# A six-layer decoder block on one core: the tokens of three groups go to the experts by way of DRAM, and the last pairs' sums use four banks

## The chip, the cores and the metric

The kernel runs on one core of a Trainium2 chip. The metric is device time in microseconds (us) of one execution; the time of a kernel is the median of several runs. The core has a matrix engine (TensorE, in the profile PE, with its weight loads as PEld), three engines for elementwise work (VectorE as DVE, ScalarE as ACT, GpSimd as POOL) and SyncE (SP), whose queue issues most of the DMAs here. Matrix products land in PSUM, which has eight banks of 128 x 512 float32; everything else lives in SBUF (128 partitions) or in DRAM.

## The reference

Two decoder layers on 16 blocks of 128 tokens with 512 features, all in float32. Each layer is self-attention, cross-attention to a context, and a feed-forward part; after each of the six, the result is added to x and a layernorm follows. The change touches the last two of them:

```python
x = _layernorm(x + _L1_xattn_ref(x, ctx_512, Wq, Wkv_expand, Wout))   # 16 heads of 32, causal softmax
x = _layernorm(x + _L1_ffn_ref(x, gate, gate_up, down, shared_gate_up, shared_down))

logits = x @ gate_weight.T                      # 8 experts
topk_w, topk_idx = top_k(softmax(logits), 2)    # two experts for each token
y = sum over the two experts e of w_e * (silu(x @ gate_e) * (x @ up_e)) @ down_e
y = y + (silu(x @ shared_gate) * (x @ shared_up)) @ shared_down
```

## The kernel before

x stays in SBUF as 16 tiles of 128 tokens x 512 features, one for each block b. Four blocks make a group, so there are four groups. A matrix product over features needs x turned, with features on partitions. The kernel has two ways to do that. `transpose_x` (line L124) uses PE: four 128 x 128 transposes into one "mm" bank and one copy by ACT (L129). The class `Turn` (L133 to L154) goes through DRAM: `send` lets ACT write a copy of x with its columns regrouped (L144) and SP write that copy to the DRAM tensor `turned` (L145); `fetch` reads it back in four DMAs (L151), such that each 32-row stripe lands on its partitions; `back` turns the 32 x 32 squares on DVE (L154). Layer 0 and the first attention of layer 1 use `Turn` for some blocks.

**The cross-attention of layer 1** is run by `attend` (L255), a software pipeline over 18 steps n. In step n it makes the scores of block n, applies the value product of block n-2 into a PSUM bank of the tag "pt" and copies it to SBUF as `oT` by ACT (L274). Then for each of four sets of heads it starts the softmax of block n (DVE: mask and maximum, L212 and L214; ACT: four exponentials, L219), finishes an earlier one (DVE reciprocal L225, POOL multiply L226), and turns the weights of block n-1 on PE into a "pt" bank (L231). At the second set, `project_out` (L172) multiplies by the output weights (L176), adds x on DVE (L177) and normalises: statistics on DVE (L111, L113), the inverse root on POOL, and the scaling of x[b] on POOL (L122). In between, `Share.deal` hands out the projections of the next group: on PE `pk`, `pq` and `pv` into two "mm" banks (L165), which are emptied as keys on DVE (L987), as queries `qT` on ACT (L991) and as values `v` on ACT (L996).

**The experts** begin at L1050. Before the router can work, all 16 blocks are turned with `transpose_x` into two tiles that each hold two groups, and SP copies x[b] to the DRAM tensor `sums` (L1054), to which the experts' results are added later. The router's logits of all four groups are accumulated in one bank (L1058); a chain of small DVE operations then gives each token two places in a list sorted by expert (`slot`, and `which`, L1158, the expert of each tile of 128 places). The shared expert's first half, `hidden` (L1102), takes one group at a time: two matrix products (L1116), Silu on ACT (L1123), product on DVE (L1124). After each of these from the second call on, `send` (L1183) copies the rows of one block on ACT (L1189) and scatters them on POOL to their places (L1194). Then 39 tiles of sorted tokens pass through their experts (L1244 to L1277), with the shared expert's second half dealt out between them.

**The end** adds up. Of blocks 8 to 15, the pairs (8,12), (9,13) and (10,14) get their shared product there by `shared_pair` (L1290): ten matmuls over two banks and one short one for each block (L1299, L1307). `add_late` (L1384) adds the experts' sums on DVE, which empties the banks. Blocks 11 and 15 follow one at a time (L165). Statistics, scaling and output follow each.

The order on each engine comes from a scheduler: it places the instructions of the program, unless `keep_in_program_order` fixes them, by its own estimate of when each can run. Once built, each engine takes its queue in that order. A DMA on SP also waits for the one eight places before it in its own ring of eight semaphores.

Of the kernel before, what the change touches and what calls it, by code (L numbers as in the profile page):

```python
# [18 lines left out]
P = 128  # L19
NB = 16  # L20
D = 512
# [25 lines left out]
def decoder_kernel(ctx: ExitStack, tc: tile.TileContext, a: dict, out: bass.AP):  # L47
# [25 lines left out]
    def bank(tag, shape, name):  # L73
        return psum.pool.tile(shape, F32, tag=tag, name=name, bufs=psum.banks[tag])
# [11 lines left out]
    def load_const(name, shape, src, pool=const):  # L86
        t = pool.tile(shape, F32, tag=name, name=name)
        nc.sync.dma_start(t, src)
        return t
# [30 lines left out]
    def layernorm(b, engine=nc.vector):  # L120
        mean, rstd = statistics(b)
        engine.tensor_scalar(x[b], x[b], mean, rstd, ALU.subtract, ALU.mult)  # L122

    def transpose_x(xT, b, at):  # L124

        tr = bank("mm", [P, KC, P], "tr")
        for k in range(KC):
            nc.tensor.transpose(tr[:, k, :], x[b][:, k * P : (k + 1) * P], ident)
        nc.scalar.copy(xT[:, :, at : at + P], tr)  # L129
# [42 lines left out]
    def project_out(oT, wo, b):  # L172

        po = bank("mm", [P, D], "po")
        for c in range(KC):
            nc.tensor.matmul(po, lhsT=oT[:, c, :], rhs=wo[:, c, :], start=(c == 0), stop=(c == KC - 1))  # L176
        nc.vector.tensor_tensor(x[b], x[b], po, ALU.add)  # L177
        layernorm(b, nc.gpsimd)
# [23 lines left out]
    class Softmax:  # L202
# [20 lines left out]
        def finish(self):  # L223
            rs = small.tile([P, 4], F32, tag="rs", name="rs")
            nc.vector.reciprocal(rs, self.sm)  # L225
            nc.gpsimd.tensor_tensor(self.p, self.p, spread(rs, P), ALU.mult)  # L226
# [25 lines left out]
            self.parts = self.part  # L252
            self.deal()

    def attend(pool, mask, wo, prepare, score, value):  # L255


        held = {}
        share = Share(prepare(0), 1)
        share.deal()  # L260
        late = []
        for n in range(NB + 2):
            if n % GB == 0 and n < NB:
                share.rest()
                share = Share(prepare(n // GB + 1), 3 * GB if n + GB < NB else 3 * GB + 6)
            if n < NB:
                sc = [bank("sc", [P, 4, P], "sc") for _ in range(4)]
                score(sc, n)
                held[n] = [Softmax(pool, sc[c], mask) for c in range(4)]
            if n >= 2:  # L270
                av = bank("pt", [P, KC, P], "av")
                value(av, n - 2, [s.pT for s in held.pop(n - 2)])
                oT = pool.tile([P, KC, P], F32, tag="oT", name="oT")
                nc.scalar.copy(oT, av)  # L274
            for c in range(4):
                if n < NB:
                    held[n][c].start()
                    late.append(held[n][c])
                if late and (len(late) > 1 or n >= NB):
                    late.pop(0).finish()  # L280
                if 1 <= n <= NB:
                    held[n - 1][c].turn()
                if c == 1 and n >= 2:
                    project_out(oT, wo, n - 2)
                else:
                    share.deal()


    GB = 4
# [49 lines left out]
    with tc.tile_pool(name="p1", bufs=1) as p1:  # L339
# [5 lines left out]
        wo = p1.tile([P, KC, D], F32, tag="wo", name="wo")  # L345
# [44 lines left out]
        for g in range(2, NG):  # L390
            blocks = slice(g * GB, (g + 1) * GB)
# [90 lines left out]
        def score(sc, n):  # L482
            qkT = groups[n // GB][0]
            toks = slice(n % GB * P, (n % GB + 1) * P)
            for j in range(4):
                for c in range(KV):
                    rows = slice(c * HD, (c + 1) * HD)
                    nc.tensor.matmul(sc[c][:, j, :], lhsT=qkT[rows, j, toks], rhs=qkT[rows, 4, toks], start=True, stop=True)

        def value(av, n, pT):  # L490
            v = groups[n // GB][1]
            for c in range(KV):
                rows = slice(c * HD, (c + 1) * HD)
                nc.tensor.matmul(av[rows], lhsT=v[:, n % GB, rows], rhs=pT[c], start=True, stop=True)

        attend(p1, mask1, wo, prepare, score, value)
        rawp.__exit__(None, None, None)
    pre_pool = tc.tile_pool(name="pre", bufs=2, reuse_waits="tile")
# [198 lines left out]
    with tc.tile_pool(name="p3", bufs=1) as p3:  # L697
# [34 lines left out]
        for g in range(NG):  # L732
            hs = []
            if g + 1 < NG:
                coming, more = inputs(g + 1)
# [31 lines left out]
            for i in range(GB):  # L767
                b = g * GB + i
                po = bank("mm", [P, D], "po")
                for f in range(NF0):  # L770
                    for n in range(2):
                        nc.tensor.matmul(  # L772
                            po, lhsT=hs[f][n][:, i * P : (i + 1) * P], rhs=w3[:, f, :],
# [10 lines left out]
    with tc.tile_pool(name="p4", bufs=1) as p4:  # L784
# [19 lines left out]
        causal = load_const("causal", [P, P], a["causal"], p5w_)  # L804
# [11 lines left out]
        coming = []  # L816
# [120 lines left out]
    with tc.tile_pool(name="p5", bufs=1) as p5:  # L937
# [15 lines left out]
        wq5, wo5 = wqo5[:, 0], wqo5[:, 1]  # L953
# [61 lines left out]
                        start=True, stop=True,  # L1015
                    )

        attend(p5, causal, wo5, prepare, score, value)
    psum.share(mm=2, sc=3, pt=2, av=1)
    p5w.__exit__(None, None, None)  # L1020

# [5 lines left out]
    with tc.tile_pool(name="p6", bufs=1, reuse_waits="tile") as p6:  # L1027
# [6 lines left out]
        def half_rows(g):  # L1034
            return slice(g % 2 * 64, g % 2 * 64 + 64)
# [8 lines left out]
        xTs = []  # L1044
        for g in range(0, NG, 2):
            pair = p6.tile([P, 2, KC, TG], F32, tag="ew", name=f"xT{g}", bufs=3)
            xTs += [pair[:, 0], pair[:, 1]]

        with tc.tile_pool(name="p6a", bufs=1, side="right", reuse_waits="tile") as p6a:


            for b in range(NB):
                transpose_x(xTs[b // GB], b, b % GB * P)
                nc.sync.dma_start(sums[b * P : (b + 1) * P, :], x[b])  # L1054
            plT = bank("av", [P, TG], "plT")
            for k in range(KC):
# [144 lines left out]
        with tc.tile_pool(name="p6r", bufs=1, side="right", reuse_waits="tile") as p6r:  # L1201
# [80 lines left out]
            def shared_down(tasks, b, then):  # L1282
                g, i = divmod(b, GB)
                chain(
                    tasks, "po", [(acts[g][:, m_, i * P : (i + 1) * P], sw_dn[:, m_, :]) for m_ in range(5)]
                    + [(halves[g // 2][half_rows(g), i * P : (i + 1) * P], sw_dn[half_rows(g), 5, :])],
                    lambda po: then(b, po),
                )

            def shared_pair(tasks, pair, then):  # L1290


                got = {}

                def whole(b, m_):
                    g, i = divmod(b, GB)
                    if m_ == 0:
                        got[b] = bank("mm", [P, D], "po")
                    nc.tensor.matmul(  # L1299
                        got[b], lhsT=acts[g][:, m_, i * P : (i + 1) * P], rhs=sw_dn[:, m_, :],  # L1300
                        start=(m_ == 0), stop=False,
                    )

                def last():
                    for b in pair:
                        g, i = divmod(b, GB)
                        nc.tensor.matmul(  # L1307
                            got[b], lhsT=halves[g // 2][half_rows(g), i * P : (i + 1) * P],
                            rhs=sw_dn[half_rows(g), 5, :], start=False, stop=True,
                        )  # L1310
                    for b in pair:
                        then(b, got[b])

                for b in pair:
                    for m_ in range(5):
                        tasks.append((0.86, lambda b=b, m_=m_: whole(b, m_)))
                tasks.append((1.0, last))
# [13 lines left out]
            tasks = []  # L1331
# [55 lines left out]
            for blocks in order:  # L1387
                tasks = []
                if blocks[0] >= EARLY and len(blocks) == 2:
                    shared_pair(tasks, blocks, add_late)  # L1390
                for b in blocks:
                    if b < EARLY:
                        tc.keep_in_program_order(nc.gpsimd.tensor_tensor(x[b], x[b], ys[b], ALU.add))
                    elif len(blocks) == 1:
                        shared_down(tasks, b, add_late)
                for _, run in tasks:
                    run()
                at = slice(0, len(blocks))
                mv = small.tile([P, 2, 2], F32, tag="mv2", name="mv2")
                for i, b in enumerate(blocks):  # L1400
                    st = small.tile([P, 6], F32, tag="st", name="st")
                    tc.keep_in_program_order(nc.vector.bn_stats(st, x[b]))
                    tc.keep_in_program_order(nc.vector.bn_aggr(mv[:, i], st))
                ve = small.tile([P, 2], F32, tag="ve2", name="ve2")
                tc.keep_in_program_order(nc.vector.tensor_scalar(ve[:, at], mv[:, at, 1], EPS, None, ALU.add))
                minus = small.tile([P, 2], F32, tag="minus", name="minus")
                tc.keep_in_program_order(nc.vector.tensor_scalar(minus[:, at], mv[:, at, 0], -1.0, None, ALU.mult))
                if behind:
                    finish(*behind.pop())
                behind.append((blocks, mv, ve, minus))  # L1410
# [126 lines left out]
```

## Time and profile before

| what | value |
|---|---|
| three runs | 2070.22, 2071.18, 2071.78 us; median 2071.18 us |
| the profiled execution | 2073.39 us |
| its span on the core | 2071.6 us |
| granted PE clock, mean | 0.992 of full |
| cross-attention of layer 1 | about 1285 to 1497 us of the span |
| start of the experts, to the first `hidden` at full rate | 1497 to 1520 us |
| tiles of sorted tokens | about 1667 to 2019 us |
| end | 2019 to 2071.6 us |

The profile is one execution. The span is what lies between its first and last instruction on the core; the execution's own time is 1.8 us longer. Rows of a timeline show the start in the span, the duration, engine, line, output and inputs; a bracket gives the idle time of the engine before the row and what ended it. Transposes of one block count as four rows, 128 x 512 matmuls in float32 as two rows each.

### The profile page before, as it was taken

The page shows a single profiled execution, that of the slowest core. Times are in us where ns is not written, and L with a number is a line of the kernel's source. Part 1 is how long each engine was busy: PE and PEld are TensorE (multiplying, and loading weights), DVE is VectorE, ACT ScalarE, POOL GpSimd, SP SyncE. Part 2 cuts the span into 40 slices and gives each one's busy share as a digit, 9 for nine tenths or more (in the row PEclk, how much of TensorE's full clock was granted, in tenths as well). Part 3 has the DMA queues.
Part 4 walks back from the last instruction along what each step waited for, and adds up shares of the span by engine and source line. Part 5 has one row for each costly group of instructions (what it writes and reads, how often), then busy time and mean ns, then how long its engine had stood idle before and what let it go on. Part 6 is the DMA issues. An engine that isn't in the chain of part 4 may idle for free.

```text
span 2071.6 us, 25330 instructions
## 1 busy us (share of the span) xinstructions
PE 2014.1 (97%) x9093; PEld 1115.7 (54%) x9093; DVE 878.6 (42%) x1763; ACT 627.6 (30%) x2107; POOL 646.8 (31%) x674
## 2 busy tenths in 40 slices
PE   8999999999999999999999999999899999999997
PEld 4555554444444458888554445555544455555552
DVE  4777732444554254432134314777731122232234
ACT  3555532333333333222310112766622200000002
POOL 6445530111211113233322113455613222223223
PEclk9999989999999999999999999999999999999999
DMA  9201231344432232001310018500023256786844
GB/s 249 78 25 40 104 124 52 104 127 137 132 117 83 66 118 71 21 11 54 143 51 22 11 34 266 204 22 21 27 66 118 87 141 178 226 237 188 247 108 168
DMA packets 155470, 221.58 MB, mean 107 GB/s; under 512 B 49616, under 2 KB 110416, under 8 KB 150608
## 3 DMA queue, kind: packets, MB, share of 16 engines
q1 hardware_dynamic: 140448, 146.51, 22.6%
q0 software_dynamic: 13792, 72.14, 11.6%
q8 instruction: 72, 1.18, 0.2%
q10 hardware_dynamic: 1104, 1.31, 0.2%
q14 instruction: 54, 0.44, 0.1%
HBM read 182.73 MB, written 72.69 MB: 123 GB/s over the span
## 4 chain that ended last, share of the span: by engine, by line
PE 85%; DMA 5%; DVE 4%; POOL 3%; ACT 2%; issue 1%; SPq 0%; POOLq 0%; DVEq 0%; ACTq 0%
PE po L649 10%; PE po L176 7%; PE pq L590 5%; PE pq L841 5%; PE pq L165 5%; PE pg L1116 4%; PE ry L1265 4%; PE po L772 4%; PE pa L745 4%; PE pb L745 4%; DMA ew<-in_l1f_w_dram,which 4%; PE rg L1244 4%; PE ru L1244 4%; PE pu L1116 3%; PE pv L851 3%; PE av L637 3%
## 5 line engine op out<-in xcount | busy, mean ns | idle before, releaser
L226 POOL TENSOR_TENSOR p<-p,rs 128x512 f32<-128x512 f32 x192 | 200.0, 1043 | 504.0 <-DVE rs L225 494.7
L649 PE MATMUL po<-mT,cc 128*128 128x512 f32 x512 | 231.5, 600 | 0.2 <-ACT cc L642 0.2
L219 ACT ACTIVATE p<-t,nmx 128x128 f32<-128x128 f32 x512 | 198.6, 390 | 34.0 <-POOL p L226 10.2
L649 PEld LDWEIGHTS po<-mT,cc 128*128 128x128 f32 x512 | 95.1, 190 | 114.3 <-issue 106.3
L219 ACT ACTIVATE p<-sc,nmx 128x128 f32<-128x128 f32 x256 | 90.2, 374 | 117.8 <-DVE nmx L214 110.4
L590 PE MATMUL pq<-xT,wqr 128*128 128x512 f32 x256 | 115.7, 593 | 2.9 <-ACT xT L129 2.9
L1214 POOL DMA_INDIRECT ew<-in_l1f_w_dram,which x39 | 40.6, 1042 | 249.1 <-PE ry L1265 182.8
L176 PE MATMUL po<-wo,oT 128*128 128x512 f32 x256 | 116.9, 600 | 0.4 <-ACT qkT L454 0.4
L1249 ACT ACTIVATE rsg<-rg 128x352 f32<-128x352 f32 x39 | 18.1, 464 | 326.4 <-PE rg L1244 310.1
L115 POOL TENSOR_SCALAR ve<-mv 128x1 f32<-128x1 f32 x80 | 18.1, 226 | 303.0 <-DVE mv L113 289.1
L1244 PE MATMUL rg<-ew,xsT 128*128 128x352 f32 x312 | 101.8, 469 | 10.4 <-DMA ew<-in_l1f_w_dram,which 9.6
L841 PE MATMUL pq<-xT,wq 128*128 128x512 f32 x256 | 110.6, 592 | 0.7 <-ACT xT L129 0.7
L1265 PE MATMUL ry<-ew,ractT 128*128 128x512 f32 (+1 forms) x234 | 106.9, 592 | 0.0
L122 POOL TENSOR_SCALAR x<-x,mv,rstd 128x512 f32<-128x512 f32 x48 | 100.5, 2094 | 4.5
L1244 PE MATMUL ru<-ew,xsT 128*128 128x352 f32 x312 | 98.7, 459 | 0.0
L219 ACT ACTIVATION_READ_ACCUMULATOR p<-t,nmx 128x1 f32 x512 | 96.1, 188 | 0.0
L233 DVE COPY pT<-pt 128x512 f32<-128x512 f32 x128 | 86.6, 679 | 19.4 <-PE pt L231 19.4
L756 POOL TENSOR_TENSOR hl<-ht,hh 128x512 fp32r<-128x512 f32 x44 | 57.4, 1306 | 108.2 <-ACT hh L754 108.2
L231 PEld LDWEIGHTS pt<-ident,p 128*128 128x128 f32 x512 | 60.0, 141 | 55.7 <-issue 41.5
L1116 PE MATMUL pg<-xT,sw_gu 128*128 128x512 f32 x192 | 86.5, 593 | 0.0
L1277 POOL DMA_INDIRECT sums<-ry,place x39 | 61.8, 1585 | 74.7 <-DMA sums<-ry,place 37.8
L1251 DVE TENSOR_TENSOR ract<-rsg,ru 128x352 f32<-128x352 f32 x39 | 20.3, 521 | 151.0 <-issue 140.4
(243 smaller groups left out, 3676.4 us busy)
## 6 DMA issues: line engine op xcount, KB each, us to landing
piece<-in_l0f_w_dram SPq DMA_DIRECT2D x48, 352.0 KB
away<-sq SPq DMA_DIRECT2D x32, 512.0 KB
pT<-away SPq DMA_DIRECT2D x128, 128.0 KB
raw<-in_l0x_raw_dram SPq DMA_DIRECT2D x8, 1728.0 KB
slots_x<-zero SPq DMA_DIRECT2D x1, 10023.0 KB
sums<-zero SPq DMA_DIRECT2D x1, 9984.0 KB
xs<-slots_x SPq DMA_DIRECT2D x156, 64.0 KB
x<-turned SPq DMA_DIRECT2D x128, 64.0 KB
```

Of the source, the lines that this page charges most:

```text
L122: engine.tensor_scalar(x[b], x[b], mean, rstd, ALU.subtract, ALU.mult)
L165: nc.tensor.matmul(got["p"], lhsT=lhsT, rhs=rhs, start=(n == 0), stop=(n == len(pairs) - 1))
L176: nc.tensor.matmul(po, lhsT=oT[:, c, :], rhs=wo[:, c, :], start=(c == 0), stop=(c == KC - 1))
L219: nc.scalar.activation(self.p[:, j, :], src[:, j, :], AF.Exp, bias=nmx[:, j : j + 1], accum_out=self.sm[:, j : j + 1])
L226: nc.gpsimd.tensor_tensor(self.p, self.p, spread(rs, P), ALU.mult)
L590: nc.tensor.matmul(pq, lhsT=wqr[:, k, cols], rhs=xT[:, k, :], start=(k == 0), stop=(k == KC - 1))
L649: nc.tensor.matmul(self.po, lhsT=self.cc[:, 4 * par + j, :], rhs=mT[h], start=(par == 0 and j == 0), stop=(par == 1 and j == 3),)
L745: nc.tensor.matmul(dst, lhsT=wt[:, k, f * P : (f + 1) * P], rhs=xs[n][:, k, :], start=(k == 0 and n == 0), stop=(k == KC - 1 and n == 1),)
L841: nc.tensor.matmul(pq, lhsT=wq4[k // 2][:, k % 2, c * P : (c + 1) * P], rhs=xT[:, k, :], start=(k == 0), stop=(k == KC - 1))
L1116: nc.tensor.matmul(dst, lhsT=sw_gu[:, k, at : at + P], rhs=xTs[g][:, k, :], start=(k == 0), stop=(k == KC - 1),)
L1244: nc.tensor.matmul(dst, lhsT=self.xT[:, k, :], rhs=gu[:, k, off : off + FE], start=(k == 0), stop=(k == KC - 1),)
L1265: nc.tensor.matmul(po, lhsT=self.actT[:mw, m_, :], rhs=dn[:mw, m_, :], start=(m_ == 0), stop=(m_ == 2))
```

## The change

It has two parts. In the cross-attention of layer 1, after `project_out` of a block of the first three groups (b below 12), the block is sent with `Turn.send`, with one buffer for the copy. At the start of the experts these twelve blocks are fetched, with four buffers, and turned on DVE; only the four blocks of the last group still go through PE. At the end, the pair (9,13) takes its two banks from the tag "pt" in place of "mm".

```diff
-    def attend(pool, mask, wo, prepare, score, value):
+    def attend(pool, mask, wo, prepare, score, value, done=None):
...
                     project_out(oT, wo, n - 2)
+                    if done is not None:
+                        done(n - 2)
...
-        attend(p5, causal, wo5, prepare, score, value)
+        coming = {}
+
+        def send5(b):
+            if b < NB - GB:
+                coming[b] = Turn(b)
+                coming[b].send(p5)
+
+        attend(p5, causal, wo5, prepare, score, value, send5)
...
+            for b in coming:
+                coming[b].fetch(p6a, bufs=4)
+                coming[b].back(xTs[b // GB][:, :, b % GB * P : (b % GB + 1) * P])
             for b in range(NB):
-                transpose_x(xTs[b // GB], b, b % GB * P)
+                if b not in coming:
+                    transpose_x(xTs[b // GB], b, b % GB * P)
                 nc.sync.dma_start(sums[b * P : (b + 1) * P, :], x[b])
...
-            def shared_pair(tasks, pair, then):
+            def shared_pair(tasks, pair, then, tag="mm"):
...
-                        got[b] = bank("mm", [P, D], "po")
+                        got[b] = bank(tag, [P, D], "po")
...
-                    shared_pair(tasks, blocks, add_late)
+                    shared_pair(tasks, blocks, add_late, ("mm", "pt")[blocks[0] % 2])
```

## The prediction

> **What bounds the kernel now.** First the page's busy shares and the chain that ended last: TensorE (PE) is busy 97% of the span and is 85% of the chain, so a change pays when it takes time from PE or ends a PE wait, and costs when it makes PE wait.
>
> ```profile
> PE 2014.1 (97%) x9093; PEld 1115.7 (54%) x9093; DVE 878.6 (42%) x1763; ACT 627.6 (30%) x2107; POOL 646.8 (31%) x674
> PE 85%; DMA 5%; DVE 4%; POOL 3%; ACT 2%; issue 1%; SPq 0%; POOLq 0%; DVEq 0%; ACTq 0%
> ```
>
> Next the timelines by engine over the cross-attention of layer 1 (about 1285 to 1497), since the new copies go into ACT's queue there. Columns: start, duration, engine, line. In each pair below POOL's layernorm of a block (L122) comes first and ACT's copy of a later block's attention output (L274) second; last is PE's set of transposes (L231) that needs the bank which that copy empties.
>
> ```profile
> 1324.42 2.10 POOL L122 TENSOR_SCALAR x<-x,mv,rstd 128x512 f32<-128x512 f32 x1
> 1323.80 0.60 ACT L991 ACTIVATE qT<-pq 128x512 f32<-128x512 f32 x1 [1.32 <-PE pq L165]
> ...
> 1339.10 2.10 POOL L122 TENSOR_SCALAR x<-x,mv,rstd 128x512 f32<-128x512 f32 x1
> 1338.27 0.59 ACT L274 COPY oT<-av 128x512 f32<-128x512 f32 x1 [1.66 <-PE av L1013]
> 1339.47 0.60 PE L231 MATMUL pt<-ident,p 128*128 128x128 f32 x4
> ...
> 1458.20 2.10 POOL L122 TENSOR_SCALAR x<-x,mv,rstd 128x512 f32<-128x512 f32 x1
> 1456.97 0.59 ACT L274 COPY oT<-av 128x512 f32<-128x512 f32 x1 [1.01 <-PE av L1013]
> ```
>
> To be seen: ACT's work, today done at once, stands close before the layernorm's end. A copy that waits for the layernorm and is queued ahead of that work holds it back.
>
> Third, the start of the experts (PE), the nearest rows for the new steps (SP's issues; source views of L154 and L144), and the end.
>
> ```profile
> 1493.10 3.70 PE L176 MATMUL po<-wqo,oT 128*128 128x512 f32 x8 [0.73 <-ACT oT L274]
> 1497.58 1.09 PE L128 MATMUL tr<-ident,x 128*128 128x128 f32 x8 [0.78 <-DVE first L1143]
> 1502.45 1.09 PE L128 MATMUL tr<-ident,x 128*128 128x128 f32 x8
> 1503.38 1.02 PE L1116 MATMUL pg<-xT,sw_gu 128*128 128x512 f32 x2
> ...
> 1043.85 3.64 SPq L151 DMA_DIRECT2D x<-turned  x8
> L154 DVE STREAM_TRANSPOSE xT<-x x32: 668/702/711, 88.9 to 1181.2; 128x512 f32<-128x512 f32 x32
> L144 ACT COPY xp<-x x24: 607/619/625, 753.3 to 1058.0; 128x512 f32<-128x512 f32 x24
>   DMA turned<-xp: 30.1, 17
> ...
> 2026.06 1.13 PE L1307 MATMUL po<-sw_dn,half 64*128 64x512 f32 x4
> 2029.74 8.85 PE L1299 MATMUL po<-sw_dn,act 128*128 128x512 f32 x20 [2.55 <-DVE x L1384]
> 2051.11 4.56 PE L165 MATMUL po<-sw_dn,act 128*128 128x512 f32 x10 [0.77 <-DVE x L1384]
> ```
>
> The fourth row of the second part says that ACT already stood idle 30.1 us ahead of such copies (L144), in 17 waits for the DMA that empties their one buffer. ACT takes its queue in order.
>
> **The change part by part.** Where things stand after the change I take from the built program's queues, which give order and waits but no times. All times are those of the trace of before; each stall moves what follows.
>
> *Part 1, twelve copies on ACT (0.62 us, 7.4 us in all) and twelve writes on SP during the attention.* The copies' own 7.4 us lie in ACT's idle time (it is about 60% busy there). What counts is whose turn they take. Copy b waits for layernorm b on POOL; queued behind it:
> - b=0: ready at 1326.52, copy to 1327.15, then qT (1323.80 today) to 1327.7. PE's second pv, today at 1324.5, needs qT's bank: **3.2**.
> - b=1: ready 1341.20, copy to 1341.85, then oT (1338.27) to 1342.45; PE's transposes of 1339.47 wait 3.0. Four exponentials (1.55) and the context copy follow on ACT, and PE's next turn, today 1341.29, waits for that until 1344.6: **3.4** in all.
> - b=5 and b=9: ready 1390.81 and 1445.84. The second of four v copies (1388.98, 1444.00) ends at 1392.05 and 1447.1; the fourth pv (today 1389.97 and 1444.99) needs its bank: **2.1** each.
> - b=10 and b=11: ready 1460.30 and 1469.30, oT (1456.97, 1465.96) ends at 1461.55 and 1470.55, PE's transposes (1457.8, 1466.8) wait 3.8. Here PE, DVE, ACT and POOL go round in a ring of 9 us without spare projections; DVE's backlog of 0.3 to 0.7 gives a little back: **3.5** each.
> - b=2, 4, 6, 8: the copy ends at or before the next oT starts (1352.25 against 1352.26; 1378.87 against 1379.44; 1407.27 against 1407.28; 1433.9 against 1434.46): nothing, though at b=2 and 6 by a hair. b=3, 7: qT 2.1 late, but PE asks for its bank 0.6 later still: nothing. If these covers go, 0.5 to 2 each.
>
> The sum is 17.8. PE idles only about 0.9 between 1325 and 1350, so there is little to make it up with. Bounds: 0 if PSUM's spare banks hide every wait, 24.2 if all of ACT's delays (3.4, 3.6, 2.1, 2.5, 2.1, 2.5, 4, 4, without the free ones) reach PE. SP's writes (0.34 to 0.42 each) wait for the copies; behind them stand only the writes of x to the sums, which nobody asks for before the experts' results. The single buffer costs nothing: the blocks are 9 to 15 us apart.
>
> *Part 2, the experts' start.* Removed: 48 transposes in 12 sets and 12 ACT copies. At 1501.48 PE is dense, with ten of sixteen sets ahead; a pair takes 0.93 (1502.45 to 1503.38), so five pairs are **4.65** gone. Added: 48 fetches on SP, which wait for the last use of the output weights (their room), the end of po at 1496.8. SP issues eight in 3.64, 0.455 each; group 0 needs sixteen, the last issued at 1496.9+15x0.455=1503.7. Landing by the nearest row (the reads of the sums, issued 2026.29, taken up by DVE at 2029.01) 2.7: 1506.4, and the turn on DVE 0.70: 1507.1. DVE is idle there (21.65 today). PE meanwhile turns only the last four blocks. So the dense part starts at 1507.15 with 4.65 less to do: 1507.15-1501.48-4.65 = **+1.0**. With 0.6 per DMA and the 4.2 from issue to landing of the write at 754.20, +4.7; with a landing of 1.2, -0.5. Behind the 48 on SP stands only the last block's write to the sums, needed long after. Groups 1 and 2 land by 1514 and 1521.5, before PE comes to them (1516.5, 1530).
>
> The router's logits need all groups, and now come some 15 us later, the expert numbers (L1158, today 1541.65) near 1552.6. The first expert weights are first used at 1667.5: covered. Row copies on ACT wait for the scatters: today 11.4 from the first scatter (1543.97) to the copy at 1555.33. Then the seven row copies ahead of the next Silu would be through near 1573, and PE needs that bank near 1581: 8 us of cover. Each us beyond it is a us of PE.
>
> *The clock.* One rule speaks against this. In the trace a stretch of small matmuls with gaps up to 1295 was followed by a granted clock of 0.70 over 1295 to 1300, and eight 128x512 matmuls took 4.28 instead of 3.60; the 2.55 of idle at 2027 left 1.00. The Trainium skill ("TensorE: Matmul & The Clock Gate", Part 1) says that an idle window of about 3.4 us halves the clock until a busy window of the same length. PE would now idle from 1502.2 to 1507.1, 4.9. By the row at 2027 nothing, by the rule half of 3.4: **1.7**. I take the rule here, since 4.9 is nearer to it than to 2.55, and nothing for the stalls of 2 to 3.5; four of these at 1.7 are in the upper end.
>
> *Part 3, the last pairs.* PE waits 2.55 before the second pair and 0.77 before the third and before the single blocks, each for the add on DVE that empties an "mm" bank. The second pair now uses the "pt" banks, empty since 2016: it starts at 2027.2, the third finds "mm" empty (adds done 2030.4), and only the wait before the single blocks stays: 2.55+0.77 = **-3.3**. The DVE adds of pair two slip to 2038.3 behind other statistics and hold nobody. Bounds: 0 and -4.1.
>
> Sum: 17.8+1.0+1.7-3.3 = **+17.2**. The profiled span of 2071.6 becomes 2088.8, its execution of 2073.39 about 2090.6; the runs' median of 2071.18 becomes **2088.4**.
>
> **The rivals.** (a) *PE's waits are covered*, the one that ends on the other side: the spare PSUM banks and PE's queued work hide ACT's delays. For it: ACT is 60% busy and delayed 2.1 without harm at b=3, 7. Against: each wait above names the very bank. It decides when the stalls of Part 1 come to less than 4.7 (4.7+1.0+1.7-3.3=4.1); at zero, 2071.18+1.0-3.3 = 2068.9 (no measurable change), 2070.6 with the clock. (b) *Half covered*, or ACT's order less binding because the layernorms come earlier: 8.9 in place of 17.8 gives 2079.5. (c) *The fetches become the bound*: 4.7 in place of 1.0 and the rows late by 3 beyond their cover: 2088.4+6.7 = 2095. For it: 512-byte pieces at one DMA per 0.455 us leave SP no slack. (d) *The tail doesn't gain*, because the adds wait for the sums' DMA: 2091.7; against it, only pair one waits for that DMA.
>
> **How the numbers follow.** Forecast 0.55, (a) 0.08, (b) 0.19, (c) 0.13, (d) 0.05. Below 2077 lies (a) and a bit of (b); above 2096 an eighth of the rest: range 2077 to 2096. A difference of 0.2% is 4.1 us, about what can be told from no change. Slower than 2075.3 are the forecast, (c), (d) and nearly all of (b): 0.91; (a) and the rest split into 0.06 the same and 0.03 faster.
>
> **What would show it.** Right: ACT's idle time ahead of L144 ended by POOL's x (L122), some 25 us in the attention; PE waiting for qT, v and oT there, six stalls of 2 to 4; the end of the attention's last po near 1514.6; PE idle about 5 between the last transpose and the first shared matmul, waiting for DVE's xT; about 3.3 less from the first late pair to the end. Wrong: PE dense through the attention, or layernorms that end before ACT comes to the copies; the fetches taking over 10 us for group 0; PE waits among the shared experts' matmuls.

## The result, and the profile after

The changed kernel takes 2091.09 us (median of four runs, 2090.31 to 2093.17), beside 2070.7 for the kernel before (four runs, 2068.75 to 2071.78). The ratio is 1.0103, with a 95% interval of 1.0088 to 1.0117: 1% slower. The profiled execution took 2091.14 us, with a span of 2089.2 and a mean PE clock of 0.986 (0.992 before).

In the changed file lines lie up to 14 further down: `qT` L991 is L993, `v` L996 is L998, the value product L1013 is L1015, the logits L1058 are L1072, the shared matmuls L1116 are L1130 and the late pairs L1299 and L1307 are L1313 and L1321. L122, L144, L154, L176, L231 and L274 stay.

The page of the changed kernel, busy time: PE has fewer matmul rows than before (9045 against 9093) and yet is busy 3 us longer.

```profile
PE 2017.1 (97%) x9045; PEld 1115.1 (53%) x9045; DVE 888.8 (43%) x1775; ACT 627.4 (30%) x2107; POOL 646.8 (31%) x674
```

The view of waits, changed kernel, from 1285 to 1530: engine and line, what it waited for, us in total, number of waits, longest wait. First ACT, then PE.

```profile
ACT xp L144 <- POOL x L122: 44.4, 12, 5.0
ACT oT L274 <- PE av L1015: 19.5, 9, 7.9
...
PE pt L231 <- ACT oT L274: 10.2, 3, 3.7
PE av L1015 <- DVE pT L233: 4.0, 8, 0.8
PE pv L165 <- ACT v L998: 3.7, 2, 1.9
PE pv L165 <- ACT qT L993: 2.7, 1, 2.7
PE tr L128 <- POOL x L122: 2.1, 1, 2.1
```

All twelve copies wait for the layernorm, 3.7 us on average, and PE waits six times for what is queued behind them on ACT: once for `qT` (2.7), three times for `oT` (10.2), twice for `v` (3.7). None of these six was there before. The timeline of the changed kernel at block 10 shows one of them link by link (start, duration, engine, line; in brackets the idle time before, and what ended it).

```profile
1470.02 2.10 POOL L122 TENSOR_SCALAR x<-x,mv,rstd 128x512 f32<-128x512 f32 x1
1472.14 0.62 ACT L144 COPY xp<-x 128x512 f32<-128x512 f32 x1 [4.37 <-POOL x L122]
1472.67 0.58 ACT L274 COPY oT<-av 128x512 f32<-128x512 f32 x1
1473.39 0.82 PE L231 MATMUL pt<-ident,p 128*128 128x128 f32 x4 [3.70 <-ACT oT L274]
1474.01 5.14 PE L176 MATMUL po<-wqo,oT 128*128 128x512 f32 x8
```

The copy is issued as soon as the layernorm ends, `oT` follows it, and PE's transposes follow `oT` after PE has stood idle for 3.70 us. The last row holds what the prediction left out: eight 128x512 matmuls that take 3.60 at full clock took 5.14.

The next view gives busy time by stretch. The stretches run from the start of one block's layernorm on POOL to the next, so each pair of rows covers the same work. Columns: stretch, length, busy us and instructions of PE, PEld, DVE, ACT and POOL, then the granted PE clock. First the kernel before, for blocks 0 to 1, 1 to 2, 5 to 6, 10 to 11, 11 to 12 and 14 to 15:

```profile
1324.42:1339.10 14.68, 14.03 (x168) 8.96 (x168) 11.02 (x23) 9.71 (x39) 6.97 (x9) 1.00 0.05 19
1339.10:1349.50 10.40, 10.16 (x49) 5.90 (x47) 7.79 (x17) 8.66 (x37) 6.96 (x7) 1.00 0.08 27
...
1388.71:1404.52 15.81, 15.48 (x128) 9.59 (x126) 10.49 (x21) 11.04 (x41) 7.97 (x8) 1.00 0.05 19
...
1458.20:1467.19 8.99, 8.41 (x91) 5.40 (x90) 8.78 (x20) 6.97 (x34) 6.93 (x8) 1.00 0.08 30
1467.19:1476.18 8.99, 8.16 (x90) 5.23 (x89) 8.78 (x20) 6.96 (x34) 6.93 (x7) 1.00 0.09 32
...
1492.41:1499.54 7.13, 5.42 (x21) 2.86 (x22) 1.61 (x6) 3.41 (x7) 2.89 (x4) 1.00 0.10 37
```

The same stretches of the changed kernel:

```profile
1322.14:1341.12 18.98, 15.95 (x168) 10.41 (x168) 11.26 (x23) 10.00 (x39) 6.97 (x8) 0.91 0.08 28
1341.12:1357.08 15.96, 13.12 (x49) 7.77 (x47) 8.06 (x17) 9.88 (x39) 6.96 (x8) 0.79 0.09 34
...
1396.29:1414.20 17.91, 15.72 (x128) 9.49 (x126) 10.46 (x21) 11.52 (x42) 7.97 (x8) 1.00 0.08 31
...
1470.02:1484.17 14.15, 10.14 (x88) 6.14 (x88) 9.18 (x21) 7.49 (x34) 6.93 (x8) 0.88 0.11 39
1484.17:1498.20 14.03, 10.10 (x91) 6.48 (x92) 8.84 (x21) 8.56 (x38) 6.93 (x7) 0.88 0.10 38
...
1514.11:1522.84 8.73, 6.93 (x20) 3.36 (x20) 1.61 (x6) 3.73 (x7) 2.88 (x3) 0.80 0.17 57
```

To be seen: where blocks 0, 1, 10 and 11 stall (2.7 to 3.7 us at a time), the clock falls to between 0.79 and 0.91 of full, and the same matmuls are busy 1.7 to 3.0 us longer. At blocks 5 and 9, whose stalls are 1.9, it stays at 1.00. Over all fifteen stretches, from block 0 to block 15, PE is busy 177.3 us against 167.0 and idle 23.4 against 8.1.

The start of the experts and the end, changed kernel, timeline of PE:

```profile
1514.79 5.31 PE L176 MATMUL po<-wqo,oT 128*128 128x512 f32 x8 [0.73 <-ACT oT L274]
...
1524.99 1.11 PE L128 MATMUL tr<-ident,x 128*128 128x128 f32 x4 [2.06 <-POOL x L122]
1530.05 1.92 PE L1072 MATMUL plT<-xT,gate 128*32 128x512 f32 x2 [3.94 <-DVE xT L154]
...
2047.13 1.13 PE L1321 MATMUL po<-sw_dn,half 64*128 64x512 f32 x4
2048.19 8.85 PE L1313 MATMUL po<-sw_dn,act 128*128 128x512 f32 x20
...
2058.03 8.85 PE L1313 MATMUL po<-sw_dn,act 128*128 128x512 f32 x20
...
2068.71 4.56 PE L165 MATMUL po<-sw_dn,act 128*128 128x512 f32 x10 [0.77 <-DVE x L1398]
```

PE comes back 9.95 us after the end of the attention's last `po` (1520.10), behind the fourth turn of group 0. In the tail the second and third pair follow without a wait; only the 0.77 before the single blocks is left.

The whole span, divided into the same five stretches in both profiles:

| stretch | before | after | difference | forecast |
|---|---|---|---|---|
| start to block 0's layernorm after the cross-attention | 1324.42 | 1322.14 | -2.3 | 0 |
| cross-attention: block 0's layernorm to block 15's | 175.12 | 200.70 | +25.6 | +17.8 |
| from there to the first routed matmul | 167.97 | 170.87 | +2.9 | +2.7 |
| tiles, to the first pair's short matmuls (L1307, L1321) | 358.55 | 353.42 | -5.1 | 0 |
| tail | 45.54 | 42.07 | -3.5 | -3.3 |
| span | 2071.6 | 2089.2 | +17.6 | +17.2 |

The sum agrees with the forecast, but two of its rows do not: the attention cost 7.8 more, and two stretches that the change does not touch gave back 7.4.

### The profile page after: what moved, and what is told of

The parts are those of the page before. It is cut to its first block, busy times and chain, and to the rows that moved or that the text cites. A ratio compares the mean times of both kernels' runs of the same rounds, so it can differ in the third digit from the quotient of the medians.

```text
span 2089.2 us, 25346 instructions
## 1 busy us (share of the span) xinstructions
PE 2017.1 (97%) x9045; PEld 1115.1 (53%) x9045; DVE 888.8 (43%) x1775; ACT 627.4 (30%) x2107; POOL 646.8 (31%) x674
## 3 DMA queue, kind: packets, MB, share of 16 engines
q0 software_dynamic: 13792, 72.14, 11.4%
## 5 line engine op out<-in xcount | busy, mean ns | idle before, releaser
L176 PE MATMUL po<-wo,oT 128*128 128x512 f32 x256 | 116.9, 600 | 0.4 <-ACT qkT L456 0.4
L122 POOL TENSOR_SCALAR x<-x,mv,rstd 128x512 f32<-128x512 f32 x48 | 100.5, 2094 | 4.5
L231 PEld LDWEIGHTS pt<-ident,p 128*128 128x128 f32 x512 | 61.1, 144 | 65.9 <-issue 51.8
L231 PE MATMUL pt<-ident,p 128*128 128x128 f32 x512 | 80.2, 282 | 11.8 <-ACT oT L274 10.2
L1130 PE MATMUL pg<-xT,sw_gu 128*128 128x512 f32 x192 | 88.2, 603 | 0.0
L214 DVE TENSOR_REDUCE nmx<-t 128x4 f32<-128x512 f32 x128 | 83.6, 676 | 0.8
```

The lines of the kernel that those rows point to most:

```text
L231: nc.tensor.transpose(pt[:, j, :], self.p[:, j, :], ident)
L1130: nc.tensor.matmul(dst, lhsT=sw_gu[:, k, at : at + P], rhs=xTs[g][:, k, :], start=(k == 0), stop=(k == KC - 1),)
```

## The experiments

The theory (A): ACT, which takes its queue in order, stands at each copy until POOL's layernorm is done, and what is queued behind it stalls PE. Its rivals: (B) the loss is at the experts' start, behind the fetches; (C) the copies and writes themselves cost it, not the wait. And a second question, since the stretches above are longer than the stalls: (D) is it the idle time that slows the matmuls after it?

The table gives the length of the last four of these stretches in the profile of every run, then the runs' median and its ratio to the runs of the kernel before that were made beside it (their medians lie between 2069.72 and 2071.86). "To routed" goes from block 15's layernorm to the first routed matmul. The runs are told of one by one below.

| run | attention | to routed | tiles | tail | median | ratio (95%) |
|---|---|---|---|---|---|---|
| before | 175.1 | 168.0 | 358.6 | 45.5 | 2070.7 | 1 |
| changed | 200.7 | 170.9 | 353.4 | 42.1 | 2091.09 | 1.0103 (1.0088 to 1.0117) |
| tail alone | 175.1 | 168.0 | 357.9 | 42.1 | 2067.42 | 0.9978 (0.9971 to 0.9985) |
| sends alone | 200.1 | 168.0 | 358.7 | 46.9 | 2096.23 | 1.0116 (1.0099 to 1.0132) |
| sent next step | 176.9 | 171.6 | 357.3 | 42.1 | 2070.48 | 0.9997 (0.9987 to 1.0006) |
| start filled | 200.1 | 171.2 | 359.3 | 42.1 | 2096.05 | 1.0126 (1.0101 to 1.015) |
| two stalls filled | 196.4 | 171.0 | 357.8 | 42.0 | 2090.04 | 1.0084 (1.0068 to 1.0099) |
| two groups | 176.2 | 163.8 | 356.9 | 42.1 | 2062.99 | 0.9957 (0.9943 to 0.9971) |
| two groups, again | 176.2 | 163.8 | 358.2 | 42.1 | 2059.75 | 0.9948 (0.9935 to 0.9961) |
| two groups, last gaps filled | 174.6 | 163.8 | 356.9 | 42.0 | 2061.36 | 0.9954 (0.9942 to 0.9966) |

Between kernels that share them, the attention repeats within 0.6 us and the start ("to routed") within about a tenth; the tile stretch does not, and single runs of one kernel lie several us apart. So the stretches can settle what the medians can't.

### The tail alone

```diff
 (the kernel before)
-            def shared_pair(tasks, pair, then):
+            def shared_pair(tasks, pair, then, tag="mm"):
...
-                        got[b] = bank("mm", [P, D], "po")
+                        got[b] = bank(tag, [P, D], "po")
...
-                    shared_pair(tasks, blocks, add_late)
+                    shared_pair(tasks, blocks, add_late, ("mm", "pt")[blocks[0] % 2])
```

> The kernel before with the last change alone: the pair (9, 13) sums in the two pt banks. Every theory of the attention says nothing here. The prediction's Part 3: 3.3 us less than before, 2070.7 - 3.3 = 2067.4. Rival: the pairs in two banks were waiting for something else, 2070.7.

Measured 2067.42, a ratio of 0.9978; the tail takes 42.1 against 45.5. Part 3 of the forecast holds, and it is the only part of the change that helps. That the median met 2067.4 to the digit is luck: the kernel before took 2071.86 on that chip, 4.4 more, of which the tail shows 3.4.

### The sends alone

```diff
 (the changed kernel)
-            for b in coming:
-                coming[b].fetch(p6a, bufs=4)
-                coming[b].back(xTs[b // GB][:, :, b % GB * P : (b % GB + 1) * P])
             for b in range(NB):
-                if b not in coming:
-                    transpose_x(xTs[b // GB], b, b % GB * P)
+                transpose_x(xTs[b // GB], b, b % GB * P)
...
-                    shared_pair(tasks, blocks, add_late, ("mm", "pt")[blocks[0] % 2])
+                    shared_pair(tasks, blocks, add_late)
```

> The kernel before with the sends alone: the twelve copies and writes in the cross-attention, whose rows nobody fetches; the experts' start turns all sixteen blocks on TensorE, the tail sums in the mm banks. Theory A (ACT's copy waits for the layernorm, and qT, oT and v wait behind it): nearly all of the loss is here, and the stalls' lower clock with it, by the layernorm of block 15, which came 23.3 us later: 2092 to 2095. Rival B (the loss is at the experts' start, behind the 48 fetches): 2073 to 2078.

Measured 2096.23. The attention is 200.1, about 0.6 less than in the changed kernel, with the same waits of ACT to the digit:

```profile
ACT xp L144 <- POOL x L122: 44.4, 12, 5.0
ACT oT L274 <- PE av L1015: 19.5, 9, 7.9
```

From block 15's layernorm to the routed matmuls it is 168.0, as before. So the loss is made in the attention and (B) is not its cause. The median is 1 us above the range expected; in the profile the tail is 1.4 longer than in the kernel before, by a clock drop of 1.7 that is read further down.

### Each send one step later

The scheduler places a copy by its own estimate of when its data is ready, so moving the call alone might leave ACT's queue as it was (no run here tries that). So the copy is also pinned behind the exponentials that ACT has been given by then.

```diff
 (the changed kernel)
-                    if done is not None:
-                        done(n - 2)
+                    if done is not None and n >= 3:
+                        done(n - 3)
...
-        def send(self, pool, tag="xp"):
+        def send(self, pool, tag="xp", pin=False):
...
-            nc.scalar.copy(xp, x[self.b].rearrange("p (k q a) -> p q k a", k=KC, q=4))
+            turn = nc.scalar.copy(xp, x[self.b].rearrange("p (k q a) -> p q k a", k=KC, q=4))
+            if pin:
+                tc.keep_in_program_order(turn)
...
-                coming[b].send(p5)
+                coming[b].send(p5, pin=True)
```

> The changed kernel with each send one block's step later, pinned behind the exponentials that ACT has been given by then, so that the layernorm has long ended when ACT comes to the copy; same copies, writes, fetches and tail. Theory A: the six stalls and their clock go, and what is left is the start (+1.0 +1.7) and the tail (-3.3): 2066 to 2072. Rival B: 2086 to 2091, nothing of the start is changed. Rival C (the copies' own 12 x 0.6 us on ACT or the 3 MB of writes cost it, not the wait): 2085 to 2091.

Measured 2070.48, no different from the kernel before, with the same twelve copies and writes as in the changed kernel. PE's waits from 1285 to 1700 in this run:

```profile
PE av L1017 <- DVE pT L235: 4.9, 8, 0.9
PE plT L1074 <- DVE xT L156: 4.1, 1, 4.1
PE tr L128 <- POOL x L122: 2.1, 1, 2.1
PE pu L1132 <- DVE act L1140: 0.8, 1, 0.8
```

The waits of `pv` for `qT` and `v` are gone, and so are those of the transposes for `oT`: no stall of the six is left. (C) falls. The attention is 176.9, 1.8 above the kernel before. Two clock drops make up more than that, 1.5 at the last `po` and 1.2 one block earlier (both in the last section); the other stretches are 1.0 shorter in sum. What stays is the second row of the waits: the start, 171.6 against 168.0.

### The experts' start, filled

```diff
 (the changed kernel)
                 if b not in coming:
                     transpose_x(xTs[b // GB], b, b % GB * P)
+                    if b >= NB - 2:
+                        fill = bank("pt", [P, KC, P], "fill")
+                        for i in range(5 if b == NB - 2 else 10):
+                            for k in range(KC):
+                                tc.keep_in_program_order(
+                                    nc.tensor.transpose(fill[:, k, :], x[i][:, k * P : (k + 1) * P], ident)
+                                )
```

> The changed kernel with TensorE kept busy in the idle time of the experts' start: 60 transposes of blocks already there, pinned ahead of and behind block 15's, into a pt bank that nobody reads. It asks what the half clock after that idle time costs. By the prediction's term 1.7 us less than the changed kernel, 2089.4; by the rows of the changed kernel's trace (2 plT at 1.92 and 8 pg at 5.29 where 0.45 each is usual) 2.7 less, 2088.4; if the clock costs nothing on the path, 2091.1, and if the transposes run past the fetched data, more.

Measured 2096.05, where 2088.4 to 2091.1 was expected, from runs between 2089.86 and 2106.99: a miss, and as a total inconclusive. The rows tell more than the total.

```profile
1526.26 4.53 PE L1073 MATMUL fill<-ident,x 128*128 128x128 f32 x40
1532.29 1.05 PE L1079 MATMUL plT<-xT,gate 128*32 128x512 f32 x2 [1.50 <-DVE xT L154]
1533.26 3.70 PE L1137 MATMUL pg<-xT,sw_gu 128*128 128x512 f32 x8
```

After the filling, two `plT` take 1.05 (1.92 in the changed kernel) and eight `pg` 3.70 (5.29): the clock is full, and 2.5 us of slow matmuls are gone. But the second fetched block was taken up by DVE 3.3 us after the first instead of 1.8, so PE came back 11.4 us after its last `po` and not 9.95; and further on PE waited 1.7 for DVE's `act`, which stood behind row copies that waited for the scatters of earlier rows. Together these ate the gain (171.2 against 170.9). In the profiles, the rest of the difference lies mostly in the tile stretch, 359.3 against 353.4, where the two programs are alike; what lengthened it is not known.

### Two of the stalls, filled

```diff
 (the changed kernel)
+                if done is not None and c == 1 and n in (13, 14):
+                    fill = bank("mm", [P, KC, P], "fill")
+                    for i in range(7):
+                        for k in range(KC):
+                            tc.keep_in_program_order(
+                                nc.tensor.transpose(fill[:, k, :], x[i][:, k * P : (k + 1) * P], ident)
+                            )
                 if 1 <= n <= NB:
                     held[n - 1][c].turn()
```

> The changed kernel with TensorE kept busy in two of the six stalls, those of blocks 10 and 11 (3.7 us each): 28 transposes of blocks already there, pinned ahead of the second pt of the step, into an mm bank that nobody reads. The stalls stay, only the idle time is filled. From block 10's layernorm to block 12's it was 17.98 before and 28.18 in the changed kernel, of which 3.7 are matmuls that ran slower than before (busy 10.14 + 10.10 against 8.41 + 8.16). Theory D (the clock falls because TensorE stood idle): 28.2 - 3.7 = 24.5. Rival (the slower matmuls have another cause, such as the copies and writes beside them): 28.2. The total moves by 3.7 at most, 2087 against 2091.

From block 10's layernorm to block 12's it took 25.06, against 28.18 in the changed kernel: 3.1 less, where 3.7 was expected of (D) and 0 of its rival. PE's timeline at block 10, then the two stretches:

```profile
1468.49 3.22 PE L286 MATMUL fill<-ident,x 128*128 128x128 f32 x28
1472.76 0.63 PE L231 MATMUL pt<-ident,p 128*128 128x128 f32 x4 [1.05 <-ACT oT L274]
...
1469.39:1481.92 12.53, 10.71 (x115) 7.77 (x114) 9.07 (x20) 7.38 (x34) 6.96 (x8) 1.00 0.12 44
1481.92:1494.45 12.53, 10.87 (x114) 7.72 (x113) 9.12 (x20) 8.04 (x36) 6.96 (x7) 1.00 0.12 44
```

PE still gets its bank only when `oT` is copied, but most of the wait is filled, and the clock is 1.00 where it was 0.88 in the changed kernel (and in the two other runs that leave these stalls open, the sends alone and the start filled). The copies and writes are all still there, so it is the idle time that slowed the matmuls after these two stalls. The total fell by 1 us or so, within its scatter.

### Two groups by way of DRAM

The start waits for group 0, the first that the shared matmuls need. Here groups 1 and 2 alone are sent, each a step later, and group 0 goes through PE again.

```diff
 (the kernel with each send a step later)
-            if b < NB - GB:
+            if GB <= b < NB - GB:
```

> The kernel of the run with each send a step later, but only groups 1 and 2 go by way of DRAM; group 0, which the first shared matmuls need, is turned on TensorE with group 3 as in the kernel before. From that run's phases (block 0's layernorm to block 15's 176.9, from there to the first routed matmul 171.6): the attention stays at 175 to 177; at the start the 4.1 us of idle time ahead of plT and its half clock (2.7) go, and 16 transposes come back (1.6): 171.6 - 5.2 = 166.4, against 168.0 before, so 2067.4 (the tail alone) - 1.6 = 2065.8. Rival C (the start is bound by the 32 fetches left, 0.508 each and 16.3 in all, and by what waits in DVE's queue behind the pinned turns): 168 to 171 for that phase, 2068 to 2071.

Measured 2062.99, and 2059.75 in a second set of runs: 0.4 to 0.5% faster than the kernel before; the tail alone had 0.2%. PE's timeline:

```profile
1500.92 1.21 PE L128 MATMUL tr<-ident,x 128*128 128x128 f32 x8 [0.35 <-ACT xT L129]
1502.06 1.04 PE L1074 MATMUL plT<-xT,gate 128*32 128x512 f32 x2
1503.04 1.12 PE L1132 MATMUL pg<-xT,sw_gu 128*128 128x512 f32 x2
1504.00 1.04 PE L128 MATMUL tr<-ident,x 128*128 128x128 f32 x8
```

There is no wait for `xT`, and the start takes 163.8, 4.1 less than before: eight sets of transposes at 0.93 a pair are 3.7. I had expected 166.4, because I took over the 2.1 that PE waits for block 15's layernorm, and the 0.8 for `act`; here PE has group 0 to do meanwhile, and no wait for `act` is left. Rival C of this run, the fetches as the bound, falls.

> The kernel with two groups by way of DRAM once more, beside the one with the ten transposes: 2063.0; from block 15's layernorm to the first routed matmul 163.8, and the last po 3.7 or 5.3.

The stretches repeat (176.2, 163.8, the last `po` 5.34); the median is 3.3 below the 2063.0 expected.

### The last gaps, filled

The kernel with two groups gets ten transposes that nobody reads, four ahead of block 15's value product and six ahead of its `po`. `fill_in(count)`, left out here, issues `count` of them into a spare "mm" bank in program order.

```diff
 (the kernel with two groups)
+                if done is not None and n == NB + 1:
+                    fill_in(4)
                 value(av, n - 2, [s.pT for s in held.pop(n - 2)])
...
+                    if done is not None and n == NB + 1:
+                        fill_in(6)
                     project_out(oT, wo, n - 2)
```

> The kernel with two groups by way of DRAM, with ten transposes of blocks already there put into the attention's last idle gaps, four ahead of the last block's av and six ahead of its po, into an mm bank that nobody reads. In that kernel, in the changed one and in the one with each send a step later the last po took 5.2 to 5.4 us, in the kernel before and two others 3.7, after the same gaps (0.51, 0.77 and 0.73 us). Theory D (the gaps' sum is what drops the clock, by where a stretch of it falls): the last po takes 3.6 to 3.7, block 0's layernorm to block 15's 174.5 instead of 176.2, and the total falls by 1.7, 2061.3 against 2063.0. Rival (the drop has nothing to do with the gaps): 176.2 and 2063.0, or more by what the transposes delay.

The last `po` took 3.70 and the attention 174.6, as (D) had it. But three of nine profiles have 3.70 there with the gaps open (last section), so this one profile does not prove that the filling did it. In the medians no gain can be seen: 2061.36 beside 2059.75 without, on the same chip, with intervals that overlap.

## Why the prediction was right, and where it was not

*Part 1, the stalls: right in mechanism and place, and nearly in size.* All six stalls stood where the prediction put them, and the blocks that it called free (2, 3, 4 and 6, 7, 8) cost nothing: from block 2's layernorm to block 5's 39.21 us in both profiles, from block 6's to block 9's 39.22. The idle time added, by stretch (length less PE's busy time, after against before), against the forecast:

| block | 0 | 1 | 5 | 9 | 10 | 11 | the rest | sum |
|---|---|---|---|---|---|---|---|---|
| forecast | 3.2 | 3.4 | 2.1 | 2.1 | 3.5 | 3.5 | 0 | 17.8 |
| added idle time | 2.4 | 2.6 | 1.9 | 2.2 | 3.4 | 3.1 | -0.2 | 15.3 |
| added busy time (slower matmuls) | 1.9 | 3.0 | 0.2 | -0.1 | 1.7 | 1.9 | 1.5 | 10.2 |

Sending a step later took all six stalls away, with the copies and writes left in place. One sign was named too low: ACT stood idle 44.4 us ahead of the copies and not some 25, because all twelve waited for the layernorm, those that held nobody back too.

*The clock: the step that failed.* The prediction allowed 1.7, once, at the start, and "nothing for the stalls of 2 to 3.5" (four times 1.7 only in the upper end of its range). In fact 10.2 us of the attention's 25.6 are slower matmuls, 8.7 at the six stalls and 1.5 at the last `po`, and filling two stalls gave 3.1 of the 3.7 at these two back. The reasoning rested on one row, an idle time of 2.55 at 2027 that left the clock at 1.00, and on the rule of the Trainium skill ("TensorE: Matmul & The Clock Gate", Part 1) of an idle window of about 3.4 us. By that rule the stalls of blocks 10 and 11, forecast at 3.5, should have been charged too: half of 3.4 is 1.7 for each, an estimate from the page, and the two of 3.70 cost 1.7 and 1.9. But the rule charges nothing for shorter gaps, and the stalls of 2.68 and 2.84 at blocks 0 and 1 cost 1.9 and 3.0; here the measurement decides. The cost is not fixed either: the same 2.84 at block 1 cost 1.7 in the run with the sends alone. The prediction's other row, the clock of 0.70 at 1295 after gaps of only 0.34 and 0.44, already spoke against a safe length. And the run with the sends alone has the place at 2027 again, where it cost 1.7 us:

```profile
2053.07 10.55 PE L1309 MATMUL po<-sw_dn,act 128*128 128x512 f32 x20 [2.25 <-DVE x L1394]
```

Before, after 2.55 of idle time, the same twenty matmuls took 8.85. So one clean row is no evidence that a gap is safe. The same page also says that the window runs free of the program, so the same gap can fall differently in it from run to run. That might be why the cost varies, but a gap of 2.25 cannot fill a window of 3.4, and no run here shows the window itself: the reason stays open.

*Part 2, the start: right in place and in sum, +2.9 against +2.7, with two terms that erred against each other.* PE came back 9.95 after its last `po`, forecast 10.3. SP issued the 48 fetches in 24.4, 0.508 each rather than 0.455; group 0 was ready in time all the same, since its last fetch landed in about 1.5 us and not 2.7 (an estimate: at that spacing it was issued at 1527.8, and DVE took it up at 1529.28). The clock cost more than the 1.7: two `plT` and eight `pg` took 7.21 and not the 4.75 that they took with the start filled, 2.5 more. That leaves 0.4 for all the rest, where 1.0 was forecast. The 8 us of cover for the late routing was too generous: the changed kernel had no such wait to speak of, but two of the runs with the same 48 fetches waited 0.8 and 1.7 for `act` there.

*Part 3, the tail: right,* -3.5 in the changed kernel and -3.4 with the tail alone, forecast -3.3.

*What made the sum come out.* The attention's excess of 7.8 was nearly cancelled by -2.3 ahead of it and -5.1 in the tiles. Of the first, 0.7 is there before the cross-attention begins, and 1.6 is the clock drop near 1295, which the profile of before has and this one has not: two `pk` and eight `pq` take 6.36 there and 4.72 here (rows in the last section). In the tiles PE was busy 1.95 less and waited 6.8 for the expert weights instead of 9.6. The 353.4 is the shortest of ten profiles; the other nine lie between 356.9 and 359.3. Whether this belongs to the changed program or to its runs stays open: two runs with the same tiles, the start and the stalls filled, had 359.3 and 357.8. So the stalls are a right mechanism, but that the total of 2088.4 was good to 2.7 us is luck: the clock's term was too small, and a counterweight that the prediction had not named made up for it.

Of the rivals, "covered" and "half covered" fell with the six stalls, and (d) fell, since the tail gained. The fetches as the bound fell too, for the kernel as a whole; but at the start they were what PE waited for, and the wait is gone in the two-group kernel.

## What to carry to other kernels

A copy on an in-order queue is priced by what it waits for and by who is queued behind it, not by its 0.62 us. Put it where its data has long been ready, and make sure that the order as built has it there: here the order as built had ACT at the copy up to 5 us before the layernorm's end. Where PE is the bound, add to each stall of 2.7 us and more a loss to the clock of more than half its length (here 8.5 us on four stalls of 12.9 in sum, and 7.5 on the same four in the run with the sends alone), and choose which tiles take a slow road by which are needed first: the group needed first belongs on the fast one.

## What the runs showed of the hardware that was not expected

The same gaps can cost nothing or 1.5 us. Ahead of the attention's last `po` PE is idle 0.51, 0.77 and 0.73 us, with short matmuls between. The first row is of the kernel before, the second of the two-group kernel, the third of the one with the gaps filled:

```profile
1493.10 3.70 PE L176 MATMUL po<-wqo,oT 128*128 128x512 f32 x8 [0.73 <-ACT oT L274]
...
1491.96 5.36 PE L178 MATMUL po<-wqo,oT 128*128 128x512 f32 x8 [0.73 <-ACT oT L276]
...
1491.22 3.70 PE L178 MATMUL po<-wqo,oT 128*128 128x512 f32 x8
```

With the gaps open, it was 3.7 in three profiles (before, the tail alone, two stalls filled) and 5.2 to 5.4 in six, among kernels whose instructions there are the same. In the slow ones the granted clock goes to 0.50 for some 3 us.

Two more places do the same. One block earlier, gaps of 0.91 and 0.84 in the kernel before were followed by a `po` of 3.60 us, and gaps of 0.89 and 0.84 in the kernel with each send a step later by one of 4.42, with a clock of 0.50 from 1481 to 1483. And near 1295 the gaps are 0.34 and 0.44 in the kernel before (first two rows), and 0.35 and 0.44 in the changed kernel (last two):

```profile
1294.71 2.08 PE L165 MATMUL pk<-ctT,wkv 128*128 128x512 f32 x2 [0.44 <-ACT xT L129]
1296.58 4.28 PE L165 MATMUL pq<-xT,wqo 128*128 128x512 f32 x8
...
1294.03 1.12 PE L165 MATMUL pk<-ctT,wkv 128*128 128x512 f32 x2 [0.44 <-ACT xT L129]
1294.99 3.60 PE L165 MATMUL pq<-xT,wqo 128*128 128x512 f32 x8
```

So the clock can be halved after gaps of less than 1 us each, when several come together with short matmuls between them, and the same gaps can also leave it alone. What decides between the two is not shown; that it depends on where in time the gaps fall is a guess which no run here tests.
